# Four graph layers on one core: member marks and member values as float32r in the first layer's member sums

## The chip, the cores and the metric

The kernel runs on one core of a Trainium2 chip. A core has a matrix engine (TensorE, PE in the profile, with its weight loads listed as PEld), a vector engine (VectorE, DVE), a scalar engine (ScalarE, ACT), a general engine (GpSimd, POOL), and a sync engine (SyncE, SP), which here only issues transfers. All of them share SBUF; TensorE writes its products to PSUM, from where DVE or ACT fetch them. The metric is the time of one execution on the device in microseconds: the median of three runs is 1881.71 us (1881.08 to 1883.15).

## The reference, cut to what matters

Four graph layers are applied in turn to x, of 8 batches, 2048 nodes and 64 features, each after a layer norm and a clipping at zero. The change lies in the first layer. There, H says which of 2048 nodes belong to which of 64 hyperedges:

```python
h = x @ W
s = leaky_relu(h @ a_node, 0.2)
alpha = softmax(where(H.T > 0, s, NEG), axis=-1)          # over the nodes of an edge
agg = einsum('ben,bnf->bef', alpha, h)                    # one vector for each edge
beta = sigmoid((h @ a_gn)[:, None, :] + (agg @ a_ge)[:, :, None])
all_he = elu(beta[..., None] * h[:, None] + (1 - beta[..., None]) * agg[:, :, None])
se = tanh(elu(agg) @ fcW + fcb) @ av
coefs1 = softmax(where(H > 0, se, NEG), axis=-1)          # over the edges of a node
g = einsum('bne,benf->bnf', coefs1, all_he)
industry = einsum('nm,bmf->bnf', adj / deg, x @ W_ind)    # neighbour sums
```

After it the layer mixes industry and g for each node and adds the result to x. Layers two to four (an attention over neighbours, three steps along the adjacency, and a sum over powers of it with weights of each node's own) follow and are not touched.

## The kernel before, in words

The first layer's function (layer0) works through stages. In the first, the input is normalized tile by tile (16 tiles of 128 nodes), turned into hn, multiplied with W_ind into Y, which is kept as a high and a low part, and summed over neighbours for the first 512 of the 2048 columns (chunk 0). In the second stage, the one around the change, chunks 1 to 3 of the neighbour sums are made by `industry`: for each chunk 8 loads of adjacency rows (`at`, L951, issued on POOL's queue into 5 buffers), and for each load 16 products of 512 columns (L1106), whose sums stay in four PSUM banks, `acc`. DVE adds the adjacency rows into `ds` for the degrees. At a chunk's end `out_of` fetches the four banks into four tiles with the tag `ev` (L1136, L1138, L1140), scales them (L1144) and stores them on SP's queue (L1132).

Between these products `industry` calls small pieces of other work, called units, one or two after each 8 products. The units are, in this order:

- `members(i)` for the 16 tiles: `begin` and `part` each make h and three scores for half of the batches (L1168, PSUM tag `ph`, two buffers), write them as a high and a low part into `hi` and `lo` (L1172, L1173) for storing in DRAM (L1185, L1186, SP's queue), and form exp(leaky_relu(s)) in `es` and h times it in `hs` (L1176 to L1179). `end` multiplies the marks `M` of this tile with `hs` into `pg` (L1191) and with `es` into `pd` (L1195), which sum over all 16 tiles. It is called one member later.
- `listing`: `ranks` (L899) and `numbers` (L919) multiply the marks `MT`, edges by nodes, with a triangle of ones and with the identity, to number the edges of each node. Its last steps write `Q` and `width`.
- `table_1` to `table_5`: agg = pg / pd, the tables `tab`, `ntab` and `etab` of each edge (high part in rows 0 to 63, low part in rows 64 to 127), and in `table_5` (L1263) the sum of exp(se) over each node's edges, from MT and `ea`.

`M`, `MT` and the marks are loaded on SP's queue after chunk 0 (L1073, L1074) and made 0 or 1 by `marks` (L1269). M holds the marks twice side by side, so that agg comes out twice, in rows 0 to 63 and 64 to 127.

The order on each engine is made when the kernel is built: a scheduler takes the instructions by their place in the program, gives out buffers as earlier holders release them, and estimates when each is ready. Instructions issued through `V`, `A`, `G` or `S` keep the program's order among themselves on DVE, ACT, POOL or SP; the plain `nc.` calls may be moved.[...] The stage after this one (from about 215 us) works on pairs of nodes and edges, with `Q`, `etab`, `tab`, `ntab` and the stored `hi` and `lo`.

In the program, FP is float32 and FR is float32r, the type that the kernel gives to the high and low parts of a split value (the low part is the value less its high part); a FP product appears as two matmul instructions in the profile, a FR product as one. The profile writes both types as f32 in matmul rows.

Of the kernel before, what the change touches and what calls it, by code (L numbers as in the profile page):

```python
# [16 lines left out]
P = 128  # L17
# [758 lines left out]
def layer0(kit, hn, x1_dram, open_early, late_tile, between):  # L776
# [21 lines left out]

    sP = ExitStack()
    lst = sP.enter_context(tc.tile_pool(name="list", bufs=1, reuse_waits="tile"))  # L800
    Q = lst.tile([P, LT, 2, E], FR, name="Q")
    slot = lst.tile([P, SLOTS], FP, name="slot")
    mid = lst.tile([P, LT], FP, name="mid")
    width = lst.tile([P, LT], FP, name="width")
# [35 lines left out]

    with ExitStack() as sA:
        ypool = sA.enter_context(tc.tile_pool(name="yf", bufs=1, reuse_waits="tile"))
        M = ypool.tile([P, NT, 2, E], FP, name="M")
        MT = ypool.tile([E, N], FP, name="MT")
        agg = ypool.tile([P, B, F], FP, name="agg")
        Wx = ypool.tile([P, P + 4], FP, name="W0x")
        a_ge = ypool.tile([P, F], FP, name="a_gef")
# [29 lines left out]
        def listing(ps):  # L877


            held = {}  # L880

            def slots():
                tmp = lst.tile([P, SLOTS], mybir.dt.int32, tag="hhi", name="iota_i", bufs=3)
                G.iota(tmp, pattern=[[1, SLOTS]], base=0, channel_multiplier=0)
                V.tensor_copy(slot, tmp)
                tri = held["tri"] = lst.tile([P, P], FP, tag="hlo", name="tri", bufs=3)
                ti = lst.tile([P, P], mybir.dt.int32, tag="hlo", name="iota_t", bufs=3)
                G.iota(ti, pattern=[[1, P]], base=0, channel_multiplier=-1)
                V.tensor_copy(tri, ti)
                nc.vector.tensor_scalar(tri, tri, 0.0, None, op0=OP.is_ge)  # L890
                small = held["small"] = lst.tile([P, 5, LT], FP, tag="hlo", name="small", bufs=3)
                held["rank"] = []

            G3 = LT // 3

            def ranks(g):
                pr = ps.tile([P, G3, E], FP, tag="ph", name="pr", bufs=2)
                for k in range(G3):
                    mm(pr[0:LN, k, :], MT[:, of(G3 * g + k)], held["tri"][0:E, 0:E], start=True, stop=True)  # L899
                rank = lst.tile([P, G3, E], FP, tag="hhi", name="rank", bufs=3)  # L900
                held["rank"].append(rank)
                nc.vector.tensor_copy(rank[0:LN], pr[0:LN])
                nc.vector.tensor_copy(held["small"][0:LN, 0, G3 * g : G3 * g + G3], rank[0:LN, :, E - 1])

            def firsts():
                deg, first, past = (held["small"][0:LN, k] for k in range(3))
                pc = ps.tile([P, LT], FP, tag="ph", name="pc", bufs=2)
                mm(pc[0:LN], held["tri"][0:LN, 0:LN], deg, start=True, stop=True)
                nc.vector.tensor_copy(past, pc[0:LN])
                nc.vector.tensor_sub(first, past, deg)  # L910

            def numbers(g):

                gs = slice(G3 * g, G3 * g + G3)
                first = held["small"][0:LN, 1, gs]
                rank = held["rank"][g][0:LN]
                pr = ps.tile([P, G3, E], FP, tag="ph", name="pm", bufs=2)
                for k in range(G3):
                    mm(pr[0:LN, k, :], MT[:, of(G3 * g + k)], ident[0:E, 0:E], start=True, stop=True)  # L919
                nc.vector.tensor_tensor(rank, rank, first[:, :, None].to_broadcast([LN, G3, E]), op=OP.add)  # L920
                nc.vector.tensor_tensor(rank, rank, pr[0:LN], op=OP.mult)
                for h in range(2):
                    nc.vector.tensor_scalar(Q[0:LN, gs, h, :], rank, -1.0, None, op0=OP.add)

            def widths():
                deg, first, past, lo = (held["small"][0:LN, k] for k in range(4))
                nc.vector.tensor_tensor(mid[0:LN], first, past, op=OP.add)
                nc.vector.tensor_scalar(mid[0:LN], mid[0:LN], -0.5, 0.5, op0=OP.mult, op1=OP.add)
                nc.vector.tensor_scalar(width[0:LN], deg, 0.5, None, op0=OP.mult)

                nc.vector.tensor_reduce(bad[0:LN, 0:1], deg, AX.X, OP.min)
                nc.vector.tensor_scalar(bad[0:LN, 0:1], bad[0:LN, 0:1], 0.5, None, op0=OP.is_lt)
                nc.vector.tensor_scalar(lo, past, SLOTS + 0.5, None, op0=OP.is_gt)
                nc.vector.tensor_reduce(bad[0:LN, 1:2], lo, AX.X, OP.max)
                nc.vector.tensor_reduce(bad[0:E, 2:3], MT, AX.X, OP.max)
                nc.vector.tensor_scalar(bad[0:E, 2:3], bad[0:E, 2:3], 0.5, None, op0=OP.is_lt)

            return [slots] + [lambda g=g: ranks(g) for g in range(3)] + [firsts] + [lambda g=g: numbers(g) for g in range(3)] + [widths]
# [18 lines left out]
        with ExitStack() as s1:  # L957
# [111 lines left out]
                    at[m // 2 + 5] = rows_of(0, m // 2 + 5)  # L1069
            kit.strict = False  # L1070
            V.tensor_copy(degs, deg0)
            for h in range(2):
                S.dma_start(out=M[:, :, h, :], in_=t["L0_gnn_H"].rearrange("(t p) e -> p t e", p=P))  # L1073
            S.dma_start(out=MT, in_=t["HT"])  # L1074

        with ExitStack() as s1:
            sb = s1.enter_context(tc.tile_pool(name="e_sb", bufs=2, reuse_waits="tile"))
# [3 lines left out]
            pd = ps.tile([P, B], FP, tag="pd", name="pd")  # L1081
            units = []
            his, loaded = [], []
            for k in range(3):
                his.append([sb.tile([P, BF_ + 2 * B], FR, name=f"{v}{k}", bufs=1) for v in ("hi", "lo")])
                for v in his[k]:
                    nc.vector.memset(v[:, BF_ + B :].bitcast(FP), 0.0)
# [64 lines left out]
            def members(i):  # L1152
# [2 lines left out]
                held = []  # L1155

                def begin():
                    hi, lo = his[i % 3]
                    es = sb.tile([P, B], FP, tag="es", name="es")
                    hs = sb.tile([P, B, F], FP, tag="hs", name="hs")  # L1160
                    held.extend((hi, lo, es, hs))
                    part(0)

                def part(j):
# [17 lines left out]
                        e4[:, :, :, None].to_broadcast([P, 2, 2, F]), op=OP.mult,  # L1182
                    )
                    if j == 1:
                        nc.sync.dma_start(out=hi_dram[i * P : (i + 1) * P, :], in_=hi.bitcast(FP))  # L1185
                        nc.sync.dma_start(out=lo_dram[i * P : (i + 1) * P, :], in_=lo.bitcast(FP))  # L1186

                def end():
                    hi, lo, es, hs = held
                    M2 = M[:, i].rearrange("p h e -> p (h e)")  # L1190
                    mm(  # L1191
                        pg.rearrange("p b f -> p (b f)"), M2, hs.rearrange("p b f -> p (b f)"),
                        start=i == 0, stop=i == NT - 1,
                    )
                    mm(pd, M2, es, start=i == 0, stop=i == NT - 1)  # L1195

                return begin, lambda: part(1), end

# [3 lines left out]
            def table_1():  # L1202
                rd = sb.tile([P, B], FP, name="rd", bufs=1)
                nc.vector.tensor_scalar_max(rd, pd, 1e-30)
                nc.vector.reciprocal(rd, rd)
                nc.vector.tensor_tensor(agg, pg, rd[:, :, None].to_broadcast([P, B, F]), op=OP.mult)


                t1 = sb.tile([P, B, F], FP, tag="hs", name="t1")
                for v, f, d in ((ntab, -0.5, 0.0), (tab, 1.0, 1.0)):  # L1210
                    nc.vector.tensor_scalar(t1, agg, f, d, op0=OP.mult, op1=OP.add)
                    nc.scalar.copy(v, t1)
                    nc.vector.tensor_tensor(v[half(1)], t1[half(1)], v[half(1)].bitcast(FP), op=OP.subtract)
                t2 = sb.tile([P, B, F], FP, tag="hs", name="t2")
                nc.vector.tensor_scalar(t2, agg, 0.0, None, op0=OP.min)
                nc.scalar.activation(t2, t2, AF.Exp)
                nc.vector.scalar_tensor_tensor(t2, t2, -1.0, agg, op0=OP.add, op1=OP.max)
                kept["t2"] = t2.rearrange("p b f -> p (b f)")

            def table_2():  # L1220
# [3 lines left out]
                for p in range(NP):  # L1224
                    nc.tensor.transpose(pt[:, p, :], kept["t2"][0:E, p * P : (p + 1) * P], ident[0:E, 0:E])
                nc.vector.tensor_copy(heT, pt)
                t3 = sb.tile([P, B, F], FP, tag="hs", name="t3")
                nc.vector.tensor_tensor(t3, agg, a_ge[:, None, :].to_broadcast([P, B, F]), op=OP.mult)
                nc.vector.tensor_reduce(ea[:, 0:B], t3, AX.X, OP.add)

# [26 lines left out]
            def table_5(part):  # L1257
# [2 lines left out]
                    kept["pn"] = ps.tile([P, LT, B], FP, tag="pd", name="pn")  # L1260
                pn = kept["pn"]
                for i in range(3 * part, 3 * part + 3):
                    mm(pn[0:LN, i, :], MT[:, of(i)], kept["ea"][0:E, B : 2 * B], start=True, stop=True)  # L1263
                if 3 * part + 3 < LT:
                    return
                nc.vector.tensor_scalar_max(rden[0:LN], pn[0:LN], 1e-30)
                nc.vector.reciprocal(rden[0:LN], rden[0:LN])

            def marks():  # L1269
                Mf = M.rearrange("p t h e -> p (t h e)")  # L1270
                V.tensor_scalar(Mf, Mf, 0.0, None, op0=OP.is_gt)
                V.tensor_scalar(MT, MT, 0.0, None, op0=OP.is_gt)

            marks()
            weights(ps, *first)
            kit.sync = nc.sync
            held = {}
# [1116 lines left out]
```

## Time and profile before

| what | value |
|---|---|
| median of 3 runs | 1881.71 us |
| the profiled execution's own time | 1880.27 us |
| its span, first to last instruction | 1878.1 us |
| PE busy in the span | 1840.7 us (98%) |
| DVE busy | 1174.5 us (63%) |
| ACT busy | 463.1 us (25%) |
| granted TensorE clock, mean | 0.996 |
| pg products (L1191) | 32 instructions, 592 ns each |
| pr, pm, pn products (L899, L919, L1263) | 36 instructions each, 264, 264 and 243 ns |

Times in the views count from the span's start. A row of a group gives busy time and the mean duration of one instruction;[...] their records overlap, and the distance between two starts says more than the duration. A row of waits gives which instruction waited, whose end it waited for, the sum, the number of times and the longest one. A row of a table of stretches gives the busy time of each engine in it. Rows in order of time give the start, the duration of the merged instructions, engine, line and operation, and how many they are.

### The profile page before, as it was taken

To read this page: it belongs to the slowest core of one execution; us is meant where nothing else is said; L and a number is where in the kernel's file an instruction comes from. 1 tells how busy PE (TensorE), PEld (TensorE's weight loads), DVE (VectorE), ACT (ScalarE), POOL (GpSimd) and SP (SyncE) were. 2 spreads that over 40 slices of the span, in tenths; PEclk is the share of its full clock that TensorE was granted. 3 is DMA by queue.
4 is the path that set the end of the run, shared out by engine and by line. 5 is a ranking of instruction groups with operands and counts; after the bars stand their busy time and mean duration, and the time that the engine had idled before them with its cause. 6 is when DMAs were issued, how large, how long until landed. Compare 5 with 4: busy or idle time off the path is not lost.

```text
span 1878.1 us, 26150 instructions
## 1 busy us (share of the span) xinstructions
PE 1840.7 (98%) x10364; PEld 1146.9 (61%) x10364; DVE 1174.5 (63%) x1843; ACT 463.1 (25%) x1048; POOL 311.7 (17%) x435
## 2 busy tenths in 40 slices
PE   8999999899999999999999999999999999999997
PEld 7877767443333333577765577855677755777653
DVE  7766699789999999932446732357523275524465
ACT  5422455572222221121301112200112101113000
POOL 4211387220000000000111200012100021101122
PEclk9999999999999999999999999999999999999999
DMA  7666395383222222142101022101122011121000
GB/s 205 186 185 207 103 284 144 107 208 79 54 61 52 63 57 57 46 99 67 51 13 28 22 69 62 34 23 26 43 62 62 12 30 28 54 65 51 5 20 12
DMA packets 86372, 142.60 MB, mean 76 GB/s; under 512 B 33800, under 2 KB 34056, under 8 KB 83568
## 3 DMA queue, kind: packets, MB, share of 16 engines
q1 hardware_dynamic: 64976, 80.64, 14.8%
q0 software_dynamic: 21040, 56.98, 12.4%
q10 hardware_dynamic: 224, 3.22, 0.5%
q8 instruction: 83, 1.36, 0.3%
q14 instruction: 49, 0.40, 0.1%
HBM read 106.85 MB, written 37.09 MB: 77 GB/s over the span
## 4 chain that ended last, share of the span: by engine, by line
PE 50%; issue 10%; DMA 2%; POOL 2%; DVE 1%; POOLq 0%; ACT 0%; SPq 0%; DVEq 0%
PE acc L737 31%; PE u L737 14%; PE py L737 2%; PE pv L737 1%; POOL fold L2281 1%; PE var L737 1%; PE mean L737 1%; DMA xd<-e 0%; DMA W3f<-in_L_gnn_weight 0%; DMA den<-d_dram 0%; PE tx L744 0%; POOL ot L2282 0%; PE tv L744 0%; PE tp L744 0%; DVE pt L1807 0%
## 5 line engine op out<-in xcount | busy, mean ns | idle before, releaser
L737 PE MATMUL acc<-aT,parts 128*128 128x512 f32 x1664 | 441.3, 409 | 0.0
L737 PEld LDWEIGHTS acc<-aT,parts 128*128 128x128 f32 x1664 | 306.6, 188 | 97.7 <-issue 39.2
L737 PE MATMUL o<-pt,hS 128*32 128x512 f32 x2048 | 247.1, 593 | 2.0 <-DVE pt L632 1.2
L737 PE MATMUL u<-W3f,y 64*128 64x512 f32 x1024 | 241.3, 589 | 0.0
L2269 DVE TENSOR_TENSOR pr<-u,embf 128x512 f32<-128x512 f32 x256 | 170.6, 687 | 109.8 <-PE u L737 103.1
L1807 DVE SCALAR_TENSOR_TENSOR pt<-R,wd,aT 128x1024 f32<-128x1024 f32 x188 | 230.0, 1276 | 8.5 <-DMA R<-r_dram 5.2
L737 PEld LDWEIGHTS u<-W3f,y 64*128 64x128 f32 x1024 | 100.0, 187 | 119.8 <-issue 119.8
L737 PEld LDWEIGHTS o<-pt,hS 128*32 128x32 f32 x2048 | 79.1, 110 | 143.8 <-issue 112.8
L737 PE MATMUL dn<-pt,vd 128*32 128x512 f32 x1024 | 134.9, 593 | 0.0
L737 PE MATMUL u<-W3f,v 64*128 64x512 f32 x512 | 133.0, 596 | 0.0
L2281 POOL TENSOR_TENSOR fold<-fold 128x256 f32<-128x256 f32 x64 | 47.8, 746 | 495.8 <-DVE fold L2280 495.8
L2060 DVE TENSOR_TENSOR yb<-py,cb_f 128x512 f32<-128x512 f32 x32 | 22.1, 691 | 157.9 <-PE py L737 157.9
L1106 PE MATMUL acc<-at,Y 128*128 128x512 f32 x384 | 101.7, 405 | 0.3 <-ACT ev L1136 0.2
L737 PE MATMUL acc<-aTl,parts 128*128 128x512 f32 x384 | 99.7, 398 | 0.0
L2157 POOL TENSOR_TENSOR bq<-bq,xp 128x512 f32<-128x512 f32 x16 | 20.7, 1293 | 421.9 <-ACT xp L2140 421.9
L2273 DVE TENSOR_TENSOR pr<-pr 128x512 f32<-128x512 f32 x128 | 88.0, 688 | 2.2
L737 PEld LDWEIGHTS u<-W3f,v 64*128 64x128 f32 x512 | 56.5, 186 | 49.6 <-issue 36.3
L1807 DVE SCALAR_TENSOR_TENSOR pt<-R,wd,aTl 128x1024 f32<-128x1024 f32 x64 | 79.3, 1280 | 8.6 <-PE dn L737 3.9
L737 PEld LDWEIGHTS dn<-pt,vd 128*32 128x32 f32 x1024 | 40.7, 110 | 67.7 <-issue 49.2
L737 PEld LDWEIGHTS acc<-aTl,parts 128*128 128x128 f32 x384 | 71.5, 188 | 16.2
L1106 PEld LDWEIGHTS acc<-at,Y 128*128 128x128 f32 x384 | 68.5, 188 | 14.1 <-issue 0.8
L2074 DVE TENSOR_TENSOR parts<-tp,parts 128x512 fp32r<-128x512 f32 x16 | 11.1, 692 | 85.3 <-ACT parts L2073 85.3
(374 smaller groups left out, 2683.0 us busy)
## 6 DMA issues: line engine op xcount, KB each, us to landing
at<-in_adjT POOLq DMA_DIRECT2D x32, 512.0 KB, 4.6
raw<-in_adjT SPq DMA_DIRECT2D x64, 256.0 KB, 3.3
aT<-in_adjT POOLq DMA_DIRECT2D x12, 1024.0 KB, 7.5
xp<-xd SPq DMA_DIRECT2D x45, 256.0 KB, 2.9
R<-r_dram SPq DMA_DIRECT2D x14, 512.0 KB, 3.8
hhi<-hi_dram POOLq DMA_DIRECT2D x18, 235.1 KB, 4.3
hlo<-lo_dram POOLq DMA_DIRECT2D x18, 235.1 KB, 4.4
hi_dram<-hi SPq DMA_DIRECT2D x16, 264.0 KB, 3.1
```

The lines of the kernel that those rows point to most:

```text
L737: one = self.nc.tensor.matmul(*args, **kw)
L1106: mm(acc[p], Y[h][:, m, p, :], at[:, k, :], start=m + h == 0, stop=m == NT - 1 and h == 1)
L1807: V.scalar_tensor_tensor(pt, R, w, a.bitcast(FP), op0=OP.max, op1=OP.mult)
L2060: nc.vector.tensor_tensor(yb, py, bias[:, None, :].to_broadcast([P, 4, P]), op=OP.add)
L2074: nc.vector.tensor_tensor(lo, tp, hi.bitcast(FP), op=OP.subtract)
L2157: nc.gpsimd.tensor_add(bq, bq, xp)
L2269: nc.vector.tensor_tensor(a, u[h], emb[:, i, 8 * w : 8 * w + 8, None].to_broadcast([P, 8, F]), op=OP.mult)
L2273: nc.vector.tensor_add(pr[h], pr[h], a)
L2281: nc.gpsimd.tensor_add(fold[:, :, 0:2, :], fold[:, :, 0:2, :], fold[:, :, 2:4, :])
```

## The change

M and MT become float32r. M's marks are loaded once into `Mraw`, which takes the place of Q until Q is first written, and written twice by one instruction with a repeated input. MT has 128 rows, the marks twice one under the other, filled by two transfers on POOL's queue in place of one on SP's. The member's values hs are split: ACT copies them to `hsh`, float32r, in a buffer of the tag `ev`, DVE subtracts that from hs into `hsl`; `end` multiplies M with both and sums them in pg. pd is made as before, with M read as float32. ranks and numbers read MT's first 64 rows as float32r, with tri and ident_r; table_5 multiplies all 128 rows of MT with etab's second half, high and low part in one product. There are two pairs of hi and lo instead of three, and one buffer of the tag hs instead of two.

```diff
-    Q = lst.tile([P, LT, 2, E], FR, name="Q")
+    Mraw = lst.tile([P, LT, 2, E], FP, tag="Q", name="Mraw")[:, 0 : NT // 2].rearrange("p t h e -> p (t h) e")
...
-        M = ypool.tile([P, NT, 2, E], FP, name="M")
-        MT = ypool.tile([E, N], FP, name="MT")
+        M = ypool.tile([P, NT, 2, E], FR, name="M")
+        MT = ypool.tile([2 * E, N], FR, name="MT")
...
-                tri = held["tri"] = lst.tile([P, P], FP, tag="hlo", name="tri", bufs=3)
+                tri = held["tri"] = lst.tile([P, P], FR, tag="hlo", name="tri", bufs=3)
...
-                    mm(pr[0:LN, k, :], MT[:, of(G3 * g + k)], held["tri"][0:E, 0:E], start=True, stop=True)
+                    mm(pr[0:LN, k, :], MT[0:E, of(G3 * g + k)], held["tri"][0:E, 0:E], start=True, stop=True)
...
-                    mm(pr[0:LN, k, :], MT[:, of(G3 * g + k)], ident[0:E, 0:E], start=True, stop=True)
+                    mm(pr[0:LN, k, :], MT[0:E, of(G3 * g + k)], ident_r[0:E, 0:E], start=True, stop=True)
...
+            S.dma_start(out=Mraw, in_=t["L0_gnn_H"].rearrange("(t p) e -> p t e", p=P))
             for h in range(2):
-                S.dma_start(out=M[:, :, h, :], in_=t["L0_gnn_H"].rearrange("(t p) e -> p t e", p=P))
-            S.dma_start(out=MT, in_=t["HT"])
+                G.dma_start(out=MT[half(h)], in_=t["HT"].bitcast(FR))
...
-            for k in range(3):
+            for k in range(2):
                 his.append([sb.tile([P, BF_ + 2 * B], FR, name=f"{v}{k}", bufs=1) for v in ("hi", "lo")])
...
-                    hi, lo = his[i % 3]
+                    hi, lo = his[i % 2]
                     es = sb.tile([P, B], FP, tag="es", name="es")
-                    hs = sb.tile([P, B, F], FP, tag="hs", name="hs")
+                    hs = sb.tile([P, B, F], FP, tag="hs", name="hs", bufs=1)
...
                     if j == 1:
+                        two = sb.tile([P, CW], FR, tag="ev", name="hsh", bufs=4), sb.tile([P, CW], FR, tag="hsl", name="hsl")
+                        hf = hs.rearrange("p b f -> p (b f)")
+                        nc.scalar.activation(two[0], hf, AF.Copy)
+                        nc.vector.tensor_sub(two[1], hf, two[0].bitcast(FP))
+                        held[3] = two
                         nc.sync.dma_start(out=hi_dram[i * P : (i + 1) * P, :], in_=hi.bitcast(FP))
...
-                    mm(
-                        pg.rearrange("p b f -> p (b f)"), M2, hs.rearrange("p b f -> p (b f)"),
-                        start=i == 0, stop=i == NT - 1,
-                    )
-                    mm(pd, M2, es, start=i == 0, stop=i == NT - 1)
+                    for k, part in enumerate(hs):
+                        mm(
+                            pg.rearrange("p b f -> p (b f)"), M2, part,
+                            start=i == 0 and k == 0, stop=i == NT - 1 and k == 1,
+                        )
+                    mm(pd, M2.bitcast(FP), es, start=i == 0, stop=i == NT - 1)
...
-                t1 = sb.tile([P, B, F], FP, tag="hs", name="t1")
+                t1 = sb.tile([P, B, F], FP, tag="hs", bufs=1, name="t1")
...
-                    mm(pn[0:LN, i, :], MT[:, of(i)], kept["ea"][0:E, B : 2 * B], start=True, stop=True)
+                    mm(pn[0:LN, i, :], MT[:, of(i)], etab[:, B:], start=True, stop=True)
...
             def marks():
-                Mf = M.rearrange("p t h e -> p (t h e)")
-                V.tensor_scalar(Mf, Mf, 0.0, None, op0=OP.is_gt)
-                V.tensor_scalar(MT, MT, 0.0, None, op0=OP.is_gt)
+                V.tensor_scalar(M, Mraw[:, :, None, :].to_broadcast([P, NT, 2, E]), 0.0, None, op0=OP.is_gt)
+                V.tensor_scalar(MT, MT.bitcast(FP), 0.0, None, op0=OP.is_gt)
 
             marks()
+            Q = lst.tile([P, LT, 2, E], FR, tag="Q", name="Q")
```

t2 and t3 of table_1 and table_2 get bufs=1 like t1. Where tri or MT is read by DVE, or by a product that stays float32 (`firsts`), it is read as float32.

More of the change, by code (lines that the diff above doesn't have):

```diff
@@ L889, in slots @@
                 V.tensor_copy(tri, ti)
-                nc.vector.tensor_scalar(tri, tri, 0.0, None, op0=OP.is_ge)
+                nc.vector.tensor_scalar(tri, tri.bitcast(FP), 0.0, None, op0=OP.is_ge)
                 small = held["small"] = lst.tile([P, 5, LT], FP, tag="hlo", name="small", bufs=3)
@@ L907, in firsts @@
                 pc = ps.tile([P, LT], FP, tag="ph", name="pc", bufs=2)
-                mm(pc[0:LN], held["tri"][0:LN, 0:LN], deg, start=True, stop=True)
+                mm(pc[0:LN], held["tri"][0:LN, 0:LN].bitcast(FP), deg, start=True, stop=True)
                 nc.vector.tensor_copy(past, pc[0:LN])
@@ L934, in widths @@
                 nc.vector.tensor_reduce(bad[0:LN, 1:2], lo, AX.X, OP.max)
-                nc.vector.tensor_reduce(bad[0:E, 2:3], MT, AX.X, OP.max)
+                nc.vector.tensor_reduce(bad[0:E, 2:3], MT[0:E].bitcast(FP), AX.X, OP.max)
                 nc.vector.tensor_scalar(bad[0:E, 2:3], bad[0:E, 2:3], 0.5, None, op0=OP.is_lt)
@@ L1213, in table_1 @@
                     nc.vector.tensor_tensor(v[half(1)], t1[half(1)], v[half(1)].bitcast(FP), op=OP.subtract)
-                t2 = sb.tile([P, B, F], FP, tag="hs", name="t2")
+                t2 = sb.tile([P, B, F], FP, tag="hs", bufs=1, name="t2")
                 nc.vector.tensor_scalar(t2, agg, 0.0, None, op0=OP.min)
@@ L1226, in table_2 @@
                 nc.vector.tensor_copy(heT, pt)
-                t3 = sb.tile([P, B, F], FP, tag="hs", name="t3")
+                t3 = sb.tile([P, B, F], FP, tag="hs", bufs=1, name="t3")
                 nc.vector.tensor_tensor(t3, agg, a_ge[:, None, :].to_broadcast([P, B, F]), op=OP.mult)
```

## The prediction

> **What bounds the kernel now.** I read four views in this order: the page's busy rows, a table of stretches of time, the PE's instructions in order of time, and the waits. The page first:
>
> ```profile
> span 1878.1 us, 26150 instructions
> ...
> PE 1840.7 (98%) x10364; PEld 1146.9 (61%) x10364; DVE 1174.5 (63%) x1843; ACT 463.1 (25%) x1048; POOL 311.7 (17%) x435
> ```
>
> TensorE is busy 98% of the span, but that is an average, and the change touches one stage. Its limits come from the PE's timeline: chunk 1 of the neighbour sums starts at 73.75 us (first L1106 product), the stage's last product ends near 214.9 us, members start at 75.6 us and the last member product is at 186.1 us. The table of stretches for the stage and for the members' part (busy us and instructions of PE, PEld, DVE, ACT, POOL, then clock, DMA share, GB/s):
>
> ```profile
> 72.30:214.90 142.60, 142.31 (x736) 112.78 (x734) 92.51 (x265) 38.96 (x123) 18.43 (x27) 1.00 0.57 170
> 76.40:186.10 109.70, 109.42 (x564) 86.63 (x563) 74.12 (x233) 28.45 (x106) 16.95 (x24) 1.00 0.70 210
> ```
>
> PE never rests here: 142.31 of 142.60 us at the full granted clock. DVE has 50 us free, ACT 104 us. So a microsecond of PE work taken out of this stage should end the stage a microsecond earlier. A busy PE in this view has overlapping records, so the price of a product is the distance between starts. From the PE's timeline (start, us, instruction, count):
>
> ```profile
> 95.73 1.41 PE L899 MATMUL pr<-tri,MT 64*114 64x64 f32 x12
> 97.07 2.10 PE L1106 MATMUL acc<-at,Y 128*128 128x512 f32 x8
> 99.01 1.06 PE L1168 MATMUL ph<-W0x,hn 128*128 128x132 f32 x8
> ...
> 101.77 1.02 PE L1191 MATMUL pg<-hs,M 128*128 128x512 f32 x2
> 102.62 0.28 PE L1195 MATMUL pd<-es,M 128*128 128x8 f32 x2
> ...
> 208.44 0.76 PE L1263 MATMUL pn<-ea,MT 64*114 64x8 f32 x6
> 209.13 0.74 PE L1127 MATMUL deg<-ds,ones_r 128*128 128x512 f32 x2
> ```
>
> A float32 product is issued as two instructions, a float32r one (acc) as one. Twelve pr instructions take 97.07-95.73 = 1.34 us, 0.112 each; eight acc take 1.94 us, 0.2425 each; a pg pair takes 0.85 us; six pn take 0.69 us, 0.115 each. Two rows of the next stage's timeline price short float32r products:
>
> ```profile
> 263.56 0.26 PE L737 MATMUL pm<-hlo,sT 114*128 114x16 f32 x1
> 263.67 0.26 PE L737 MATMUL pm<-etab,oT 128*128 128x16 f32 x1
> ```
>
> 0.11 us each with 128 weight columns: as much as one of the two instructions of a short float32 product[...].
>
> Last, who waited in 60 to 215 us (total, times, longest):
>
> ```profile
> POOL at L951 <- PE acc L1106: 46.4, 10, 6.5
> ACT hi L1172 <- PE ph L1168: 39.9, 22, 4.9
> ```
>
> The adjacency loads wait for PE to free buffers, and ACT waits for PE: PE sets the pace of both.
>
> **The change, part by part.**
>
> *pg (L1191), 16 nodes' tiles.* One float32 product (0.85 us) becomes two float32r products, high and low. By the stage's own acc row they cost 2 x 0.2425 = 0.485, saving 0.37 x 16 = 5.9 us.[...] The row has 242 ns under the same weight loads, so I take 5.9[...]. pd (L1195) stays float32 by its bitcast: no change.
>
> *ranks and numbers (L899, L919).* 36 + 36 instructions of 0.112 us become 18 + 18 of 0.11: 36 x 0.112 = 4.0 us saved.[...]
>
> *table_5 (L1263).* 36 instructions become 18. They now load 128 rows instead of 64; the pm rows show 128 rows at 0.11, so the doubled marks are free: 18 x 0.113 = 2.0 us saved. These products now wait for etab's low half (a DVE subtract of 0.17 us after a 0.20 us ACT copy) instead of ea.
>
> Sum on PE: 5.9 + 4.0 + 2.0 = 11.9 us.
>
> *New work on ACT and DVE.* Per tile a 128x512 copy to float32r (0.62 us by the ACT row Y<-py) and a subtract (0.69 us by the DVE row Y<-py,Y): 9.9 us on ACT, 11.0 us on DVE, inside 104 and 50 free us: hidden. DVE has the in-order adjacency sums (1.22 us each, 21 of them), so the part's DVE load rises to about 85 of the 100 us that would be left: covered, not by much.
>
> *hs with one buffer.* Member i+1 may write hs once member i's copy and subtract are done. A member's chain from its first copy to its last hs is 99.66 to 102.5 = 2.85 us; with 0.62, 0.69 and one 1.22 sum in between 5.4 us. PE's pace after the change is (186.1-9.9-76.4)/16 = 6.24 us per member: hidden by 0.8 us. In table_1 to table_3, t1 and t2 now take turns in the one buffer: t2's first step, at 188.25, moves behind t1's last, at 192.15, so 3.9 us later; with etab's subtract 4.4 us. Cover: the first pn was at 202.4, 16.3 us after the last member product. Now that is 176.2 + 16.3 + 4.4 = 196.9, pn done at 198.9, against PE's end of stage at 214.9-11.9 = 203.0. 4.1 us to spare; past that each us counts fully.
>
> *his from three pairs to two.* Tile i+2 writes hi once tile i's stores have landed. Stores landed in 3.5 us at the median (8.4 at most); two tiles are 12.5 us: hidden.
>
> *hsh in the ring of ev.* Four buffers are shared by a chunk's four ev tiles and the members' hsh. At a chunk's end an ev copy frees the PSUM that the next chunk's first products need, and hsh needs an ev whose store has landed. The SP queue in order of time shows the late place:
>
> ```profile
> 125.06 1.23 SPq L632 DMA_DIRECT2D ivc_f<-L_gnn_intervention_value  x2
> 126.39 1.00 SPq L1132 DMA_DIRECT2D ind_dram<-ev  x2
> 127.49 0.40 SPq L1185 DMA_DIRECT2D hi_dram<-hi  x1
> 127.98 0.38 SPq L1186 DMA_DIRECT2D lo_dram<-lo  x1
> 128.46 1.40 SPq L1132 DMA_DIRECT2D ind_dram<-ev  x2
> ```
>
> Products written at 121.5 to 122.9 are stored only behind 9.5 us of layer-2 loads and land 3.2 us later, 129.6 to 133; hs of the member there is ready at 126.8. So its hsh waits about 3 us, and behind it on ACT stand the next member's hi copies, for which a PSUM buffer and PE's next ph wait. Bounds: 0 (PE has acc products to go on with) to 6.3 us (133.1-126.8, all exposed). At the second boundary stores went out at 172.6 to 177.2 and no member waits that long. I take 0.6 at each boundary: 1.2 us lost.
>
> *Loads and marks.* M's two SP loads become one, MT's single SP load becomes two on POOL's queue. The marks cost the same DVE time where M's broadcast input keeps the rate (1.215 us), up to 2.27 (the reduce L935 over as many elements) where not: 1.1 us inside DVE's 1.3 to 1.5 us pauses at 62 to 68.[...] (min/median/max ns):
>
> ```profile
> L951 POOL DMA_DIRECT2D at<-in_adjT x32: 706/716/1032, 1.3 to 188.5; - x32
> ```
>
> The 1032 is the issue at 63.69, under M's marks. By the row two issues lose 0.6 us[...]. MT goes out behind the last centring (56.6) and ahead of the iotas (57.63), lands within its old 10.8 us, by 69, where its marks stood at 66.7. Behind them in DVE's fixed order stand W0x's copies, needed at 75.6, and the acc evacuations at 72.3, which PE waits for. Zero is taken; were MT put behind the load at 63.69, it lands near 77 and costs 4 to 5 us.
>
> Forecast: 11.9 - 1.2 = 10.7 us off the span, 1878.1 to 1867.4. Later stages follow PE and start earlier by as much. This execution took 1880.27, 2.2 around its span; the median of runs, 1881.71, lies 1.4 above. Median: 1871.0.
>
> **Rivals.**
> *B, the shared ring costs.* Both boundaries stall PE for 2 to 4 us: 4 to 8 us lost, 1874 to 1878. For it: the SP backlog. Against: PE's other work is at hand. 22%.
> *C, more is gained.*[...] 8%.
> *D, slower: the members' chain takes over.* Place: the single hs buffer, DVE between sums. The stage ends at 76.4 + 16T + 20.7 + 2.0 with T us per member. At T = 6.5 PE's gain begins to go, at 7.24 all is gone, at 7.47 it is slower than before by 0.2%; T = 8 gives 1894. Against: 5.4 worked out, and 50 free us of DVE. For: the chain's waits between ACT and DVE. 10%: 3% no change, 7% slower.
> *E, no effect: the adjacency loads set the stage.* Loads land in 4.6 us and are asked four ahead, while PE takes over 5 us each. 4%, 1882.
>
> **How the numbers follow.** Likeliest 56%: 1869 to 1873. Tell-apart bound 0.2%, 3.8 us: 1878 or less is faster. Faster: 56 + 8 + 20 of B's 22 = 84%; same: 2 + 3 + 4 = 9%; slower 7%. Leaving out D, E and B's end gives 1866.5 to 1878.
>
> **What will show it.** pg as two products 0.48 us apart in all; pr, pm, pn with 18 instructions each; PE still without gaps from 73 to 203; the next stage's first px at 203 instead of 215.1. Wrong, if PE shows idle before acc or pg on hsl, hsh or ev, if pn moves to the stage's end with PE waiting, or if MT's marks stand behind their load after 72 us.

## The result and the profile after

| kernel | median, us | lowest to highest | runs |
|---|---|---|---|
| before | 1881.51 | 1878.98 to 1883.37 | 12 |
| after | 1877.98 | 1875.28 to 1879.55 | 12 |

After takes 0.9976 of the time of before (95% interval 0.9968 to 0.9983): 3.5 us faster by the medians, 3.2 to 6.0 by the interval, where 10.7 were forecast. Nineteen more runs of the changed kernel in the last experiment gave 0.9968 (0.9951 to 0.9985) and 0.9975 (0.9966 to 0.9983). The profiled execution took 1879.05 us, its span 1877.3. The busy row of its page:

```profile
PE 1835.9 (98%) x10310; PEld 1139.9 (61%) x10310; DVE 1183.8 (63%) x1857; ACT 472.2 (25%) x1064; POOL 313.2 (17%) x437
```

PE has 54 instructions fewer: 18 each from pr, pm and pn. In the PE's order of time the products have the prices forecast (before's rows stand in the prediction):

```profile
96.28 0.75 PE L899 MATMUL pr<-tri,MT 64*114 64x64 f32 x6
96.96 2.12 PE L1106 MATMUL acc<-at,Y 128*128 128x512 f32 x8
...
101.66 0.39 PE L1197 MATMUL pg<-hsh,M 128*128 128x512 f32 x1
101.89 0.39 PE L1197 MATMUL pg<-hsl,M 128*128 128x512 f32 x1
102.13 0.28 PE L1201 MATMUL pd<-es,M 128*128 128x8 f32 x2
...
204.58 0.67 PE L1269 MATMUL pn<-etab,MT 128*114 128x8 f32 x6
205.11 2.09 PE L1106 MATMUL acc<-at,Y 128*128 128x512 f32 x8
```

Both pg halves take 102.13 - 101.66 = 0.47 us, where one float32 product took 0.85. Six pr, one group of six node tiles, take 0.68 us here and 0.71 in the other groups that neither a pause nor a low clock touches, where their twelve took 1.34. Six pn, now one per tile and not half of one, take 0.53 us, 0.09 each. The sum by these prices: 16 x 0.38 = 6.1 for pg, 6 groups x (1.34 - 0.71) = 3.8 for pr and pm, 36 x 0.115 - 18 x 0.09 = 2.5 for pn: 12.4 us saved.

The stage, from its first L1106 product to the first px, didn't get shorter by that. Before, it ran from 73.75 to 215.1 us, 141.4 long; after, from 75.36 to 212.4, 137.1 long: 4.3 us less. (In the twelve profiles of this document the stage starts anywhere from 72.8 to 76.7 us; three profiles of the changed kernel alone span that range. So lengths are compared, not ends.) The table of stretches, one row for the stage of each kernel, before first (length, then busy us and instructions of PE, PEld, DVE, ACT, POOL, then granted clock, DMA share, GB/s):

```profile
73.75:215.10 141.35, 141.02 (x729) 111.62 (x727) 91.53 (x265) 38.38 (x123) 18.63 (x27) 1.00 0.56 169
```

```profile
75.36:212.40 137.04, 133.21 (x675) 109.78 (x673) 99.85 (x281) 47.80 (x139) 18.71 (x27) 0.96 0.58 174
```

Two things are new: PE is idle for 137.04 - 133.21 = 3.8 us, where it was idle for 0.3, and the clock is 0.96, where it was 1.00. The idle time is found at the two chunk ends inside the stage. Before, PE in order of time at the first end, and the stretches from the degree product to the first product of the next chunk, at the first end and at the second:

```profile
118.56 0.62 PE L1127 MATMUL deg<-ds,ones_r 128*128 128x512 f32 x2
119.01 1.08 PE L1106 MATMUL acc<-at,Y 128*128 128x512 f32 x4
119.93 0.61 PE L1168 MATMUL ph<-W0x,hn 128*128 128x132 f32 x4
120.38 1.02 PE L1191 MATMUL pg<-hs,M 128*128 128x512 f32 x2
...
122.16 2.34 PE L1106 MATMUL acc<-at,Y 128*128 128x512 f32 x9 [0.19 <-ACT ev L1136]
```

```profile
118.56:122.16 3.60, 3.42 (x19) 2.60 (x17) 2.51 (x6) 2.21 (x6) 0.72 (x1) 1.00 0.49 150
167.56:172.64 5.08, 4.98 (x31) 3.79 (x30) 3.58 (x9) 2.69 (x7) 0.78 (x2) 1.00 0.56 179
```

After, the same place (a bracket gives the idle time ahead of the row and what ended it):

```profile
115.57 2.09 PE L1106 MATMUL acc<-at,Y 128*128 128x512 f32 x8
117.50 0.39 PE L1197 MATMUL pg<-hsh,M 128*128 128x512 f32 x1
117.73 0.39 PE L1197 MATMUL pg<-hsl,M 128*128 128x512 f32 x1
...
118.20 0.70 PE L1127 MATMUL deg<-ds,ones_r 128*128 128x512 f32 x2
118.74 0.61 PE L1168 MATMUL ph<-W0x,hn 128*128 128x132 f32 x4
120.28 0.72 PE L1168 MATMUL ph<-W0x,hn 128*128 128x132 f32 x4 [0.93 <-DVE bad L1120]
121.78 3.78 PE L1106 MATMUL acc<-at,Y 128*128 128x512 f32 x9 [0.78 <-DVE ev L1140]
```

From the degree product to the next chunk's first acc it is 3.6 us in both kernels at the first end: deg, DVE's rdeg (L1117), ACT's Ln and Exp (L1118, L1119), then DVE's ev (L1140), which empties the first PSUM bank. At the second end it is 5.1 us before and 4.3 after; DVE's work on rank and Q lies in between there. This chain was there before too, and hardly showed among the waits, because PE had four acc, eight ph and a float32 pg to do meanwhile (and twelve pm at the second end): it was idle for 3.60 - 3.42 = 0.2 us and 5.08 - 4.98 = 0.1 us, so the chain was just covered, with nothing to spare. After, the last acc and both pg halves are already done when deg comes, and eight ph are left. The second ph must also wait 0.93 us for DVE's minimum over the degrees (L1120), since deg lies in ph's ring of two PSUM buffers.

Why deg comes that late against PE's other work is in DVE's order of time, before first:

```profile
116.65 0.43 DVE L1179 TENSOR_TENSOR hs<-ph,es 128x256 f32<-128x256 f32 x1 [0.27 <-ACT es L1178]
116.99 1.22 DVE L632 TENSOR_TENSOR ds<-ds,at 128x1024 fp32r<-128x1024 f32 x1
```

After:

```profile
116.23 0.69 DVE L1188 TENSOR_TENSOR hsl<-hs,hsh 128x512 fp32r<-128x512 f32 x1 [0.70 <-ACT hsh L1187]
116.84 1.22 DVE L632 TENSOR_TENSOR ds<-ds,at 128x1024 fp32r<-128x1024 f32 x1
118.94 0.69 DVE L1117 TENSOR_SCALAR rdeg<-deg 128x512 f32<-128x512 f32 x1 [0.88 <-PE deg L1127]
...
121.03 0.69 DVE L1140 TENSOR_TENSOR ev<-acc,rdeg 128x512 f32<-128x512 f32 x1 [0.41 <-ACT rdeg L1119]
```

Before, the last degree sum ds follows the member's hs at once. After, the new subtract hsl stands ahead of it, and waits 0.70 us for ACT's hsh; deg needs ds. The two ends of after, each followed by the stretch of low clock behind it, in the table of stretches:

```profile
118.20:121.78 3.58, 1.87 (x12) 1.40 (x11) 2.43 (x7) 2.31 (x6) 0.72 (x1) 1.00 0.63 175
122.31:125.73 3.42, 3.42 (x10) 2.21 (x8) 2.66 (x10) 0.67 (x4) 0.00 (x0) 0.50 0.07 3
166.42:170.75 4.33, 2.59 (x16) 1.92 (x17) 3.49 (x9) 2.68 (x7) 0.78 (x2) 0.92 0.77 238
170.10:176.93 6.83, 6.18 (x17) 5.02 (x18) 4.14 (x14) 2.48 (x10) 1.84 (x2) 0.50 0.77 245
```

PE idles 3.58 - 1.87 = 1.7 us at each end, and then the granted clock is 0.50, for 3.4 us at the first end and for 6.8 us at the second, where it falls inside the second pause. The nine acc behind the first end take 3.71 us (121.78 to 125.49), where nine at full clock take 2.2 to 2.3 (rows of other kernels below).

### The profile page after: what moved, and what is told of

It reads as the page before. It is cut to its first block, busy times and chain, and to the rows that moved or that the text cites. A ratio compares the mean times of both kernels' runs of the same rounds, so it can differ in the third digit from the quotient of the medians.

```text
span 1877.3 us, 26090 instructions
## 1 busy us (share of the span) xinstructions
PE 1835.9 (98%) x10310; PEld 1139.9 (61%) x10310; DVE 1183.8 (63%) x1857; ACT 472.2 (25%) x1064; POOL 313.2 (17%) x437
## 2 busy tenths in 40 slices
DMA packets 84388, 142.60 MB, mean 76 GB/s; under 512 B 31752, under 2 KB 32008, under 8 KB 81520
## 4 chain that ended last, share of the span: by engine, by line
PE 50%; issue 10%; DMA 2%; POOL 2%; DVE 1%; POOLq 0%; ACT 0%; SPq 0%; DVEq 0%
PE acc L737 31%; PE u L737 14%; PE py L737 2%; PE pv L737 1%; POOL fold L2287 1%; PE var L737 1%; PE mean L737 1%; DMA den<-d_dram 0%; DMA xd<-e 0%; DMA d_dram<-ds 0%; PE tx L744 0%; DMA W3f<-in_L_gnn_weight 0%; PE tv L744 0%; PE tp L744 0%; POOL ot L2288 0%
## 5 line engine op out<-in xcount | busy, mean ns | idle before, releaser
L737 PEld LDWEIGHTS o<-pt,hS 128*32 128x32 f32 x2048 | 75.1, 110 | 148.9 <-issue 122.9
L1106 PE MATMUL acc<-at,Y 128*128 128x512 f32 x384 | 105.6, 417 | 1.8 <-DVE ev L1140 1.8
L1106 PEld LDWEIGHTS acc<-at,Y 128*128 128x128 f32 x384 | 71.3, 195 | 16.0 <-DVE ev L1140 2.2
```

The source lines that it names most:

```text
L737: one = self.nc.tensor.matmul(*args, **kw)
L1106: mm(acc[p], Y[h][:, m, p, :], at[:, k, :], start=m + h == 0, stop=m == NT - 1 and h == 1)
```

## The experiments

Theory 1, **the chunk ends**: the degree chain is no longer covered, and the gaps and the clock behind them take what the products saved. Theory 2, **the ring**: hsh's place among the ev buffers, which the prediction charged. Theory 3, **DVE is too full** in this stage. A last rival, **the marks**: that pr, pm and pn bring less than worked out. A table of the stage in all kernels comes at the end of this part. Ratios are to the kernel before, run beside them on the same chip.

**e_copy: the banks emptied without the degrees.** Banks 0 and 2 are copied out unscaled at the chunk ends inside the stage, and scaled afterwards, as banks 1 and 3 are anyway. This takes the chain off the way to the next acc.

```diff
-                    elif rdeg is None:
+                    elif rdeg is None or c < NCW - 1:
                         nc.vector.tensor_copy(ev[p], acc[p])
...
-                return [lambda p=p: shares(p) for p in (1, 3)]
+                return [lambda p=p: shares(p) for p in ((1, 3) if c == NCW - 1 else range(NP))]
```

> The changed kernel, with the four acc banks of chunks 1 and 2 fetched as plain copies as soon as their last product is done, and multiplied with the inverse degree later (in the kernel before and in the changed one, banks 0 and 2 are fetched by a multiplication that waits for the inverse degree). Theory 1, the chunk ends: in the changed kernel PE runs out of work for some 2 us between the degree product and the first fetch (118.7 to 121.8 and 167.8 to 170.8 us), and then runs at half clock for 3.5 to 6 us; together about 8 us of the 11.9. Without that wait both gaps go and the clock stays up: 1869 to 1871. Theory 2, the ring: hsh waits for the stores of ev, which here are later still: 1878 or more. Theory 3, DVE is too full: it gets 2.8 us more work: 1878 to 1881.

1870.01 us (1868.74 to 1872.36, 5 runs), ratio 0.9941 (0.9928 to 0.9955). PE in order of time:

```profile
117.03 0.63 PE L1127 MATMUL deg<-ds,ones_r 128*128 128x512 f32 x2
117.49 0.61 PE L1168 MATMUL ph<-W0x,hn 128*128 128x132 f32 x4
117.86 1.42 PE L1106 MATMUL acc<-at,Y 128*128 128x512 f32 x5
...
119.51 3.02 PE L1106 MATMUL acc<-at,Y 128*128 128x512 f32 x12
```

No gap stands behind deg, and the stage is 128.8 us long: 12.6 less than before's, where 12.4 were worked out from the prices. The gain had been there and was lost at the chunk ends. DVE does four multiplies more in the stage than in after, so theory 3 falls.

**e_copy_before: the same edit on the kernel before.** Its diff is that of e_copy.

> The kernel before, with the same plain copies at the ends of chunks 1 and 2 as e_copy. Theory 1: the kernel before covers the wait for the degree chain with four acc products and a pg product, and loses only 0.4 to 0.5 us at each of the two ends: 1880.5 to 1881.5, no more than 1 us faster than before. If the copies gave 4 us or more here too, the chunk ends would have been as bad before, and they would not explain where the gain went.

1882.11 us (1880.21 to 1885.27, 13 runs), ratio 1.0003 (0.9995 to 1.0011), 0.6 us over the range expected. Before, the chain was covered, so taking it away brings nothing. The 12 us of e_copy are therefore the change's own, not a second gain on top.

**e_ring: a buffer of its own for hsh.**

```diff
-                        two = sb.tile([P, CW], FR, tag="ev", name="hsh", bufs=4), sb.tile([P, CW], FR, tag="hsl", name="hsl")
+                        two = sb.tile([P, CW], FR, tag="hsh", name="hsh", bufs=1), sb.tile([P, CW], FR, tag="hsl", name="hsl")
```

> The changed kernel, with hsh in one buffer of its own instead of the ring of ev. Theory 1: the wait of hsh for the stores goes (3.3 us on ACT at 124 to 127 us), but PE did not wait for it, so the gaps and the halved clock stay: 1877 to 1879. Theory 2: 1870 to 1873. Theory 3: 1877 to 1879.

1875.46 us (1873.79 to 1878.04, 8 runs), ratio 0.9971 (0.9961 to 0.9982): 2.5 us under after in the medians, lower than theory 1 had it, but the two intervals overlap. Its first product behind the first end:

```profile
122.30 2.34 PE L1106 MATMUL acc<-at,Y 128*128 128x512 f32 x9 [0.73 <-DVE ev L1140]
```

Ahead of it, ph waits 0.93 us for L1120, as in after. The gaps are the same, so the ring doesn't make them. But here the clock stayed at 1.00, and the stage took 132.6 us. That left two readings: the shared buffer makes the clock fall in some roundabout way, or the fall comes in some executions and not in others. e_again1 and e_again2 below tell them apart.

**e_pool: the subtract hsl on POOL**, to take it from DVE's order.

```diff
-                        nc.vector.tensor_sub(two[1], hf, two[0].bitcast(FP))
+                        nc.gpsimd.tensor_sub(two[1], hf, two[0].bitcast(FP))
```

> The changed kernel, with the subtraction that makes hsl on POOL instead of DVE. Theory 1: the last degree sum of a chunk no longer stands behind the copy and the subtraction in DVE's order (1.3 us), the degree product comes 1.3 us earlier, PE's gap falls from 2 us to under 1 us and the clock does not fall: 1871 to 1874. Theory 2, the ring: no change, 1877 to 1879. Theory 3, DVE too full: 11 us less on it, 1868 to 1872, with the gain spread over the stage and not at the two chunk ends.

1875.53 us (1872.36 to 1878.95, 6 runs), ratio 0.9964 (0.9952 to 0.9976): less than expected. The waits of PE in 70 to 215 us (total, times, longest) say why:

```profile
PE acc L1106 <- DVE ev L1140: 1.8, 2, 1.0
PE pg L1197 <- POOL hsl L1188: 1.2, 2, 0.9
```

The wait of ph on L1120 is gone, since deg now comes ahead of the last acc and pg; that of acc on ev stays; and pg waits 1.2 us for POOL, where the subtract takes 1.41 and 1.45 us (the two next to the first end) and not 0.69. But 0.9 of these 1.2 us, and 0.7 us of pg's first half just ahead of them, lie at 130 to 132 us, behind an hsh that waited 2.38 us for the store of an ev tile: there the ring and POOL act together. One wait was traded for others, and the ratio can't be told from the changed kernel's (0.9968 and 0.9975 in e_again1 and e_again2).

**e_late: the subtract one unit later**, so that it no longer stands ahead of the last ds. The amount of work is the same; only the order on DVE, and what the scheduler makes of it, differs.

```diff
-                        nc.vector.tensor_sub(two[1], hf, two[0].bitcast(FP))
                         held[3] = two
+                        held.append(hf)
...
-                    hi, lo, es, hs = held
+                    hi, lo, es, hs = held[0:4]
+                    nc.vector.tensor_sub(hs[1], held[4], hs[0].bitcast(FP))
```

> The changed kernel, with hsl's subtraction called in a member's last step instead of its second, so that in DVE's order the degree sums can stand ahead of it. All work is the same. Theory 1: at the first chunk end the degree product is then followed by two acc products, pg's two and pd before PE waits, about 1 us of gap instead of 2 at each end: 1873 to 1876. If the gap had nothing to do with this order: 1877 to 1879.

1873.24 us (1870.52 to 1873.61, 5 runs), ratio 0.9953 (0.9939 to 0.9967). DVE at the first chunk end, and the stretch from deg to acc:

```profile
113.73 1.22 DVE L632 TENSOR_TENSOR ds<-ds,at 128x1024 fp32r<-128x1024 f32 x1
114.86 0.68 DVE L1195 TENSOR_TENSOR hsl<-hs,hsh 128x512 fp32r<-128x512 f32 x1
115.97 0.69 DVE L1117 TENSOR_SCALAR rdeg<-deg 128x512 f32<-128x512 f32 x1 [0.43 <-PE deg L1127]
```

```profile
115.31:118.90 3.59, 2.73 (x18) 2.27 (x16) 2.85 (x9) 2.20 (x7) 0.72 (x1) 1.00 0.52 166
```

With ds ahead of hsl, two acc and both pg halves fall behind deg, PE idles 0.86 us at this end and not 1.7, and the nine acc behind it take 2.27 us. The chain is still 3.59 us. By the medians this is 4.7 us under after, but only 1.4 and 4.4 us under the changed kernel's later runs (e_again1 and e_again2 below). So part of the loss is an order that can be had otherwise at no cost, and the rest is the chain.

**e_marks: the marks' products alone.** pg is one float32 product again, with no hsh and hsl and with two buffers of hs; ranks, numbers and table_5 stay as changed.

```diff
-                    for k, part in enumerate(hs):
-                        mm(
-                            pg.rearrange("p b f -> p (b f)"), M2, part,
-                            start=i == 0 and k == 0, stop=i == NT - 1 and k == 1,
-                        )
+                    mm(
+                        pg.rearrange("p b f -> p (b f)"), M2.bitcast(FP), hs.rearrange("p b f -> p (b f)"),
+                        start=i == 0, stop=i == NT - 1,
+                    )
```

> The changed kernel without the split of the members' values: pg is one float32 product again (M read as float32), no hsh and hsl, two buffers of hs; ranks, numbers and table_5 stay as changed (128-row marks, float32r). It saves 4.0 + 2.0 = 6.0 us on PE. Theory 1, the chunk ends: pg's halves and the copy and subtraction behind them make the gap at a chunk's end; here PE has four acc products and a float32 pg behind the degree product as in the kernel before, no gap over 0.5 us, the clock stays: 1875 to 1876.5. Rival, the marks: if the gap comes from the marks' conversion (less work for PE anywhere in the chunk lets it reach the chunk's end ahead of DVE), both gaps are there and it is 1878 to 1882.

1873.38 us (1872.88 to 1876.07, 5 runs), ratio 0.9960 (0.9946 to 0.9973), which is 7.5 us less than before (5.1 to 10.2), more than expected. The stage is 6.6 us shorter; pr, pm and pn by the prices measured bring 3.8 + 2.5 = 6.3. The last rival falls. PE at the first end is as in before, with cover behind deg and no gap over 0.23 us:

```profile
119.71 0.62 PE L1127 MATMUL deg<-ds,ones_r 128*128 128x512 f32 x2
120.17 1.08 PE L1106 MATMUL acc<-at,Y 128*128 128x512 f32 x4
...
121.54 1.02 PE L1191 MATMUL pg<-hs,M 128*128 128x512 f32 x2
...
123.36 2.35 PE L1106 MATMUL acc<-at,Y 128*128 128x512 f32 x9 [0.23 <-ACT ev L1136]
```

**e_pg: pg's halves alone.** ranks, numbers and table_5 as before, in float32; pg as changed.

```diff
-                    mm(pr[0:LN, k, :], MT[0:E, of(G3 * g + k)], held["tri"][0:E, 0:E], start=True, stop=True)
+                    mm(pr[0:LN, k, :], MT[0:E, of(G3 * g + k)].bitcast(FP), held["tri"][0:E, 0:E].bitcast(FP), start=True, stop=True)
...
-                    mm(pn[0:LN, i, :], MT[:, of(i)], etab[:, B:], start=True, stop=True)
+                    mm(pn[0:LN, i, :], MT[0:E, of(i)].bitcast(FP), kept["ea"][0:E, B : 2 * B], start=True, stop=True)
```

> The changed kernel with ranks, numbers and table_5 in float32 as before (64 rows of MT, ident, ea); pg in two float32r products as changed. It saves 5.9 us on PE. Theory 1: it has both gaps at the chunk ends and the clock falls behind them, 4 to 8 us lost: 1880 to 1884, as slow as before. Rival, the marks: no gaps, 1875 to 1877.

1882.21 us (1880.29 to 1884.98, 13 runs), ratio 1.0001 (0.9992 to 1.0009). The edit that was to bring 5.9 us brings none. Its stage is as long as before's (141.75 against 141.35 us), with 2.9 us of idle time. At the first end ph waits 0.93 us for L1120, as in after, and then acc:

```profile
123.22 3.92 PE L1106 MATMUL acc<-at,Y 128*128 128x512 f32 x9 [0.78 <-DVE ev L1140]
```

The clock falls behind both ends (0.86 in the mean from 116 to 128 us, 0.88 from 166 to 180); at the second, a single pause of 0.92 us stands ahead of the fall. So the loss comes with pg's split, and is about as large as its gain.

**e_again1 and e_again2: the changed kernel as it is**, for two more profiles: does the clock fall in every execution?

> The changed kernel as it is, for a second profile: does the clock behind the chunk ends fall in every execution? Theory 1 (the gaps are fixed by the order of the instructions, the clock's answer to them is not): from the first L1106 product to the first px, PE idles 3.7 to 3.9 us again, with deg to acc 3.5 to 3.6 us at the first end; PE's busy time there is anything from 128.9 (clock 1.00, stage 132.6) to 133.2 us (clock 0.96, stage 137.0), and the execution's time moves with it: about 1875 with the clock held, about 1879 with two falls. Rival (the fall belongs to the buffer that hsh shares, since with a buffer of its own it did not come): busy 133 us, clock 0.96, stage 137 again.

> The same once more, a third profile. Theory 1: idle time 3.7 to 3.9 us again, busy time between 128.9 and 133.2 us, not always the same. Rival (the shared buffer): 133 us of busy time and a stage of 137 us each time.

1874.60 us (1871.72 to 1879.36, 6 runs) and 1877.60 us (1875.61 to 1879.09, 13 runs). The stretches of e_again1, from deg to acc and over the nine acc, at the first end and at the second:

```profile
115.57:119.15 3.58, 1.88 (x11) 1.39 (x10) 2.42 (x7) 2.30 (x6) 0.71 (x1) 1.00 0.63 162
119.15:121.43 2.28, 2.28 (x10) 1.61 (x10) 2.28 (x11) 0.99 (x4) 0.00 (x0) 1.00 0.26 57
163.32:167.65 4.33, 2.60 (x17) 1.93 (x17) 3.49 (x9) 2.68 (x7) 0.78 (x2) 1.00 0.79 235
167.65:171.23 3.58, 3.58 (x9) 2.76 (x10) 2.95 (x11) 1.26 (x4) 1.80 (x2) 0.57 0.66 222
```

The time from deg to acc and PE's busy time in it are after's to 0.01 us. The clock holds at the first end and falls at the second; e_again2 does the same (nine acc in 2.28 us and, at the second end, in 4.03). Theory 1's part on the clock holds: in this stage the order of PE, DVE and ACT is the same in all three executions, the clock's answer isn't. The rival, which had 133 us of busy time each time, falls: it is 130.5 and 131.8. Two things were wrong in the expectation. The execution's time doesn't follow the clock in this stage: the two profiled executions took 1874.19 and 1879.09 us, and their stages are 0.8 us apart; 3.9 us of the difference is where the stage starts (72.83 and 76.73). And the idle time is more: 4.7 us and 4.2 us, not 3.7 to 3.9. A wait is there that after didn't have. PE and ACT of e_again1 behind the first end:

```profile
128.30 0.69 PE L1168 MATMUL ph<-W0x,hn 128*128 128x132 f32 x4 [0.90 <-DVE hs L1179]
```

```profile
124.96 0.63 ACT L1187 ACTIVATE hsh<-hs 128x512 fp32r<-128x512 f32 x1 [3.31 <-DMA ind_dram<-ev]
```

This is the ring that the prediction named: hsh waits 3.31 us on ACT for an ev tile's store, hi and hs of the next member stand behind it, and the next ph waits 0.90 us for a PSUM buffer. In after the same hsh waited 3.33 us and that ph didn't wait; there the clock had been 0.50 from 122.31 to 125.73 us and slowed PE ahead of it. In e_ring hsh waits 0.73 us, for its own hs, and no ph waits on hs.

**e_copy_ring: e_copy and e_ring together.**

> The changed kernel with the plain copies at the ends of chunks 1 and 2 (as e_copy) and hsh in a buffer of its own (as e_ring). Theory 1: e_copy had one wait of PE for hsh left (0.46 us at 126.9 us); without it 1869 to 1870.5, within 1 us of e_copy. Theory 2, the ring: 3 us or more below e_copy.

1869.35 us (1866.83 to 1871.08, 5 runs), ratio 0.9931 (0.9918 to 0.9945), the fastest of all; it lies 0.7 us under e_copy, which these runs can't tell from nothing. Its stage idles 0.2 us, e_copy's 0.6.

The stage of every kernel, from the table of stretches, in us (idle is the length less PE's busy time; the clock is the mean granted one):

| kernel | length, us | idle | busy | clock |
|---|---|---|---|---|
| before | 141.35 | 0.33 | 141.02 | 1.00 |
| e_copy_before | 140.67 | 0.05 | 140.62 | 1.00 |
| e_pg | 141.75 | 2.93 | 138.82 | 0.98 |
| after | 137.04 | 3.83 | 133.21 | 0.96 |
| e_again2 | 136.05 | 4.24 | 131.81 | 0.97 |
| e_again1 | 135.23 | 4.70 | 130.53 | 0.99 |
| e_marks | 134.78 | 0.50 | 134.28 | 1.00 |
| e_pool | 133.47 | 4.09 | 129.38 | 1.00 |
| e_ring | 132.55 | 3.70 | 128.85 | 1.00 |
| e_late | 131.85 | 2.83 | 129.02 | 1.00 |
| e_copy | 128.76 | 0.63 | 128.13 | 1.00 |
| e_copy_ring | 127.93 | 0.18 | 127.75 | 1.00 |

Read against e_copy, after loses 137.04 - 128.76 = 8.3 us: 3.83 - 0.63 = 3.2 idle, and 133.21 - 128.13 = 5.1 because the same 675 or so instructions run slower, which is half of the 3.42 + 6.83 us at a clock of 0.50. In e_again1 and e_again2 the loss is 6.5 and 7.3 us. One execution's length is good to about 2 us, as the three of the changed kernel show; the medians of the runs go the same way (after 1877.98, e_copy 1870.01: 8.0 us). Nor is the stage the whole: after's profile is 4.3 us shorter in the stage than before's, but only 0.8 us in its span, since it took 1.6 us more ahead of the stage and 1.8 us more behind it. The part behind the stage takes from 1662 to 1668 us in the twelve profiles. It is longest in e_pool, 1667.6 us: the mean clock of its profiled execution is 0.993, with 1.00 in the stage, where before's is 0.996.

## Why the prediction was wrong

**"PE never rests here", so that a microsecond taken out ends the stage a microsecond earlier.** This is the step that failed, at the two chunk ends inside this stage. The 142.31 of 142.60 busy us showed that PE had no slack; they did not show what lay hidden under its work. The chain from deg to ev was in before's trace at each chunk end (3.6 and 5.1 us), with four acc and a pg over it. At the first end the float32 pg that was made cheaper was itself a quarter of that cover (0.86 of 3.42 us). What the runs showed in its place: the stage gets 12.6 us shorter with the chain out of the way (e_copy), and 4.3 us with the chain in it (after). The prediction asked what covers each added piece of ACT and DVE work, and never what was covered by the PE work that goes away.

**The PE sum, 11.9 us.** Right: 12.4 by the prices measured, 12.6 as the stage of e_copy shows it. pg is 0.47 against 0.485 forecast, pr and pm bring 3.8 against 4.0; pn is 0.09 against 0.11 and brings 2.5 instead of 2.0. The trace's row for acc was the right price for pg. Rival C, more gained, was an estimate that no row shows: even the acc<-aT products of before start 0.224 us apart or more, and at that price pg would have brought only 32 x (0.2425 - 0.224) = 0.6 us more than forecast.

**"hsh in the ring of ev ... I take 0.6 at each boundary: 1.2 us lost."** The ring wait exists at the place named, the first boundary, with about the length named (3.3 us on ACT, 3 forecast), and costs PE 0.9 us in two of three profiles and nothing in the third, nothing at the second boundary. So the term was of about the right size for what it described. But it was the only loss charged at the chunk ends, and the degree chain there cost 3.2 us of idle time and, in this profile, 5.1 more by the clock: 8.3 in place of 1.2. In the other two it is 6.5 and 7.3, with the ring's 0.9 in them.

**"hidden" for the DVE work.** By amount it was: 99.85 of 137 us busy. By place it wasn't: 0.69 us of hsl and its 0.70 us of waiting stand ahead of ds in DVE's order, and set back deg and the chain behind it. e_late, with the same work in another order, idles 0.86 us there instead of 1.7.

**The rest held.** hs with one buffer and his with two pairs cost PE no wait of their own: its waits on hs appear only behind the ring's. MT's marks and M's took 1.217 and 1.216 us, the rate kept, and stood at 68.3 and 64.9 us, ahead of what PE needs; pn ran at 203 to 205 with PE not waiting for it. Rivals D and E didn't come: e_copy's stage gives the whole saving back, so neither the members' chain nor the adjacency loads set it.

**The forecast's form.** The result, 1877.98, lies inside the range, 0.02 us under its upper end, and 7 us above the median forecast. That is luck: it is rival B's time, not its cause. B's "shared ring" had the chunk ends right, and about the worth of 4 to 8 us, by the wrong mechanism. What was named as the sign of a wrong prediction, PE idle before acc, is what the trace shows, though on ev after the degree chain and not after a store.

What stays open: why the scheduler put hsl ahead of the last ds; and how often the clock falls, known here only from three profiles of the changed kernel (both ends, second end, second end) and one each of e_pg (both), e_ring, e_pool and e_late (neither).

## What to carry to other kernels

Before work is taken off the engine that is always busy, look under it: at each place where an accumulation ends and its banks must be emptied, time the chain from the last product to the next chunk's first one, and count how much of the bounding engine's work is issued behind the chain's start. If the change shortens or moves that work so far that the chain lies bare, the gain ends there, and the pause can cost more than its own length (after against e_copy: 3.2 us more idle time, and 5.1 us more by the clock). New work on an engine with half its time free can still do harm by where it stands in that engine's order, so look at what is queued behind each added instruction at these places.

## What the runs showed of the hardware

A pause can be followed by a stretch of low clock longer than itself: behind pauses of 0.67 to 1.07 us, one or two of them at a chunk end, the granted clock was 0.50, in after for 3.41 us at the first end and 6.83 us at the second, so that nine products took 3.58 to 4.03 us instead of 2.2 to 2.3. That was so at both ends in after and e_pg and at the second end in e_again1 and e_again2. Behind pauses of like length the clock stayed at 1.00 at the first end in e_again1 and e_again2 (nine products in 2.28 us each) and at both ends in e_ring (2.26 and 2.20 us).

What decides between the two, the traces do not show. PE's busy time ahead of a fall alone does not: from deg to the next acc at the first end PE is busy for 1.87 of 3.58 us in after, where the clock fell, and for 1.88 of 3.58 us in e_again1, where it held.

In e_ring, where the clock held, the stage is 132.55 - 128.76 = 3.8 us longer than in e_copy, with 3.70 - 0.63 = 3.1 us more idle time. In after, where it fell, the stage is 8.3 us longer with 3.2 us more idle time, about two and a half times as much.
